# Scores of two tiles from seven block products: a fused cross-attention and feed-forward layer, re-ordered on all five engines

## The chip, the cores and the metric

The kernel runs on one core of a Trainium2 chip. The time is that of one execution on the device, in microseconds (us), the median of several runs. The core has five engines with instruction queues of their own: TensorE (PE; its weight loads are shown as PEld and overlap its matmuls), VectorE (DVE), ScalarE (ACT), GpSimd (POOL) and SyncE (SP), which here issues every DMA. Each queue is worked off strictly in order; semaphores tie the queues together.

## The reference

The input x has 8 batches of 1024 rows of 512 values; every batch has a context of 64 rows of 384 values. All is float32. Layer normalisation is without weights, and the linear layers of the second half quantise their input per row and their weights to -1, 0, 1.

```
def _xattn(x, context, Wq, Wk, Wv, Wo, bo):            # 8 heads of 64
    q, k, v = x @ Wq, context @ Wk, context @ Wv        # split into heads
    attn = softmax(einsum('bhsd,bhld->bhsl', q, k) * 64 ** -0.5)
    return merge_heads(einsum('bhsl,bhld->bhsd', attn, v)) @ Wo + bo

def _act_quant(x):
    scale = 127.0 / clip(max(abs(x), axis=-1), 1e-05)
    return clip(round(x * scale), -128.0, 127.0) / scale

def _bitlinear(x, w):
    return einsum('bsi,oi->bso', _act_quant(x), _weight_quant(w))

x = x + _xattn(_layernorm(x), ctx_768, Wq, Wk, Wv, Wo, bo)
h = silu(_bitlinear(_layernorm(x), w_gate)) * _bitlinear(_layernorm(x), w_up)   # 2048 wide
x = x + _bitlinear(h, w_down)
```

## The kernel before

**Tiles.** The 8192 rows are 64 tiles of 128 rows, 8 to a batch. `att[i]` is the attention of tile i, `ffn[i]` its feed-forward part, `pairs[i]` the tiles 2i and 2i+1.

**Attention through folded weights.** Context and weights are multiplied once per batch into two 512 x 512 float32 matrices: `score_w[b]` (x to the scores of 8 heads x 64 context rows) and `value_w[b]` (probabilities to the output). Three rooms hold each kind in turn, so those of later batches are made in the middle of the run, two batches at a time, in 8 steps each (`score_products`, `value_products`, L233 and L252, with copies by ScalarE). A tile's attention is then: transpose x, `scores` (four float32 matmuls of 512 columns, L360, each in two passes), subtract the maximum (L375, L377), exponentials (L382), sums and reciprocals (L386, L388), probabilities (L392), transpose them, and multiply by `value_w`. The transposes go through DMA: `split` (L310) separates the 16-bit halves on GpSimd, a DMA transpose follows (L312), and `join` (L319) puts the halves together, on ScalarE for x and on GpSimd for the probabilities p.

**Seven products for a pair's output.** Two tiles side by side are a 2 x 2 block problem: left blocks are pieces of p of 128 rows x 256, right blocks those of `value_w[b]`, 256 x 256. `Pair.product` (L454) computes the eight block products as seven, from five sums of left blocks (`Pair.sum`, L452, GpSimd, 128 x 256 each) and from sums of the weight blocks made once per batch (`value_sum`, L430, L432 and L434 on GpSimd, L436 on VectorE). The products x1 to x4 pile up in one PSUM bank, z1 and z2 in another, y goes to the bank of z; after each product VectorE adds or subtracts the bank's content as it stands into a quarter of a tile's x (L479). So x2 can't start before x1's result has been read, nor x3 before x2's, x4 before x3's, z1 before y's, z2 before z1's.

**Feed-forward.** `stats` (L282, L284, on VectorE; then L289, L291, the inverse deviation, on GpSimd), `normalise` (L493), `scale_x` (L499 and three small ones), `quantise_x` (ScalarE rounds, L509; GpSimd shrinks to 16 bits, L513; DMA transpose). `gate_up(s)`, for s from 0 to 3: four fp8 matmuls for the gate and four for the up part (L536, 512 columns), then silu on ScalarE (L551), product on VectorE (L552), and after s = 1 and s = 3 the largest value of 1024 columns (L564). `scale_h` and `quantise_h` (L577, L579, DMA transpose in two halves), and `output`, the down product (16 matmuls, L587; result added by L591).

**The order of the work.** A list written by hand brings the weights in and the first six tiles through attention. Then the loop `for k in range(NU + 1)`, NU = 64, emits step k in one order that holds for all engines; nothing re-orders it. Step k runs the feed-forward part of tile k, the quantisation of tile k + 1, the down product of tile k - 1, and the scores and softmax of tile k + 6; x of tile k + 7 is transposed. Output products of a pair are spread over two steps, y, x1, z1, x2 in the even and x3, z2, x4 in the odd one. Each step switches ScalarE's function table to Exp and back to Silu (L890, L904). From step 53 on there are exceptions: `quantised(k)` prepares two tiles in steps 53, 54, 56 and 58 and none in some others, and `downs(k)` puts the down products one step later. Gate, up and down results take turns over six PSUM banks, the block products have two of their own.

Of the kernel before, what the change touches and what calls it, by code (L numbers as in the profile page):

```python
# [29 lines left out]
def xattn_ffn_kernel(  # L30
# [58 lines left out]
    six = const.tile([P, 2, P], F32, name="p_sum_6")  # L89
# [24 lines left out]
    p_sums = [sums_room[:, i].rearrange("p (c t) -> p c t", c=2) for i in range(4)] + [six]  # L114
    value_sums = [
        [sums_room[:, ts(2 + 3 * i + j, 2)] for j in range(3)] for i in range(2)
    ]
# [169 lines left out]
    def inverse_std(mv, name, gain):  # L287
        ve = small.tile([P, 1], F32, tag="ve", name=f"ve_{name}")
        nc.gpsimd.tensor_scalar(ve, mv[:, 1:2], EPS, gain, ALU.add, ALU.mult)  # L289
        rs = small.tile([P, 1], F32, tag="rs", name=f"rs_{name}", bufs=8)  # L290
        nc.gpsimd.tensor_tensor(rs, ve, neg_half, ALU.pow)  # L291
        return rs
# [15 lines left out]
    def split(src, name):  # L308
        halves = apool.tile([P, 2, D], U16, tag=f"{name[0]}2", name=f"split_{name}")
        nc.gpsimd.tensor_copy(halves, src.bitcast(U16).rearrange("p (d h) -> p h d", h=2))  # L310
        halves_t = apool.tile([P, 2 * ND, P], U16, tag=f"{name[0]}2_t", name=f"split_t_{name}")
        nc.sync.dma_start_transpose(out=halves_t, in_=halves.rearrange("p h d -> p (h d)"))  # L312
        return halves_t

    def join(copy, halves_t, name):
        whole = apool.tile(
            [P, ND, P], F32, tag=f"{name[0]}_t", name=f"{name[0]}_t_{name}", bufs=1 + (name[0] == "p")
# [8 lines left out]
    class Attention:  # L326
# [9 lines left out]
        def copy_x(self):  # L336
            self.x_t = apool.tile([P, ND, P], F32, tag="x_t", name=f"x_t_{self.name}")
            nc.scalar.copy(self.x_t, self.pt)

        def split_x(self):  # L340
            self.x = x_tile(self.i)
            self.x2_t = split(self.x, f"x_{self.name}")
# [4 lines left out]
        def split_p(self):  # L347
            self.p2_t = split(self.p.rearrange("p h l -> p (h l)"), f"p_{self.name}")
# [16 lines left out]
        def softmax(self, between):  # L365
            self.less_maximum()
            self.exponentials()
            between()
            self.sums()
            self.probabilities()  # L370

        def less_maximum(self):
            pm = self.pm.rearrange("p (h l) -> p h l", h=HEADS)
            mx = small.tile([P, HEADS], F32, tag="mx", name=f"mx_{self.name}")
            nc.vector.tensor_reduce(mx, pm, AX.X, ALU.max)  # L375
            self.p = apool.tile([P, HEADS, L], F32, tag="p", name=f"p_{self.name}", bufs=2)
# [46 lines left out]
    def block(b, i, j):  # L423
        return value_w[b][:, ts(i, 2), ts(j, 2 * P)]

    def value_sum(b, i):

        s6, s1, s7 = value_sums[b % 2]
        if i == 0:
            nc.gpsimd.tensor_tensor(s6, block(b, 0, 0), block(b, 0, 1), ALU.add)  # L430
        elif i == 1:
            nc.gpsimd.tensor_tensor(block(b, 0, 1), block(b, 0, 1), block(b, 1, 1), ALU.subtract)  # L432
        elif i == 2:
            nc.gpsimd.tensor_tensor(s1, block(b, 1, 1), s6, ALU.subtract)  # L434
        else:
            nc.vector.scalar_tensor_tensor(s7, s1, -1.0, block(b, 1, 0), ALU.mult, ALU.subtract)  # L436

    class Pair:
        def __init__(self, i):
            self.tiles = att[2 * i], att[2 * i + 1]  # L440
            self.b, self.name, self.banks = self.tiles[0].b, f"pair{i}", {}

        def p(self, t, i):
            return self.tiles[t].p_t[:, ts(i, 2), :]

        def sum(self, i):
            p11, p12, p21, p22 = (self.p(t, i) for t in range(2) for i in range(2))
            a, b, op = (
                (p11, p21, ALU.subtract), (p11, p22, ALU.add), (p11, p12, ALU.add),
                (p22, p12, ALU.subtract), (p21, p22, ALU.add),  # L450
            )[i]
            nc.gpsimd.tensor_tensor(p_sums[i], a, b, op)  # L452

        def product(self, which):  # L454
            s6, s1, s7 = value_sums[self.b % 2]
            p, w, first = {
                "x1": (self.p(0, 0), block(self.b, 0, 1), True),
                "x2": (p_sums[1], s1, False),
                "x3": (self.p(1, 1), s7, False),
                "x4": (p_sums[3], block(self.b, 1, 0), False),  # L460
                "z1": (p_sums[0], block(self.b, 0, 0), True),
                "z2": (p_sums[4], s6, False),
                "y": (p_sums[2], block(self.b, 1, 1), True),
# [4 lines left out]
            for c in range(2):  # L468
# [3 lines left out]
                )  # L472
            t, n, op = {
                "x1": (0, 1, ALU.add), "x2": (1, 1, ALU.add), "x3": (1, 0, ALU.subtract),
                "x4": (0, 0, ALU.subtract), "z1": (1, 0, ALU.subtract), "z2": (1, 1, ALU.add),
# [6 lines left out]
    class FeedForward:  # L482
# [90 lines left out]
        def quantise_h(self):  # L573
            self.hq_t = hq_t_rooms[self.i % 2]
            for i in range(2):
                h = self.h[i]
                nc.scalar.activation(h, h, AF.Identity, bias=magic, scale=self.scale)  # L577
                hq = hq_rooms[i]
                nc.gpsimd.tensor_scalar(  # L579
                    as_chunks(hq), in_chunks(h), -MAGIC, 1.0, ALU.add, ALU.mult  # L580
                )
                nc.sync.dma_start_transpose(out=self.hq_t[:, ts(i, NF // 2), :], in_=hq)
# [267 lines left out]
    loaded = LEAD // 2 + 1  # L850
# [3 lines left out]
    def quantised(k):  # L854
# [5 lines left out]
        return [NU - 2] if k == NU - 4 else []  # L860
# [12 lines left out]
    rounds["product"] = rounds["bank"]  # L873
    for k in range(NU + 1):
        f = ffn[k] if k < NU else None
        a = att[k + LEAD] if k + LEAD < NU else None
        prev = att[k + LEAD - 1] if k == 0 else None
        after = att[k + LEAD + 1] if k + LEAD + 1 < NU else None
        quant, extra = ([ffn[i] for i in quantised(k)] + [None, None])[:2]
        pair = pairs[(k + LEAD - 2) // 2] if 2 <= k <= NU - LEAD + 1 else None  # L880
        parts = [("y", "x1", "z1", "x2"), ("x3", "z2", "x4")][k % 2] if pair else ()
        if k % 2 == 0 and loaded < NU // 2:
            load_x(loaded)
            loaded += 1
        if quant:
            quant.stats()
        if k > 0 and a:
            ffn[k - 1].quantise_h()
        if a:
            nc.scalar.preload_act_table(AF.Exp)  # L890
        if after:
            if k > 0:
                after.split_x()
            after.stats()
        if a:
            a.scores(every)

        def part(i):
            return pair.product(parts[i]) if i < len(parts) else lambda: None

        def between():
            if k == 0:
                after.copy_x()
            nc.scalar.preload_act_table(AF.Silu)  # L904
            read()
            if quant:
                quant.normalise()

        if k == 0:
            prev.transpose_p()  # L910
            prev.copy_p()
            after.transpose_x()
        if a:
            read = part(0)
            a.softmax(between)
            a.split_p()
        elif quant:
            quant.normalise()
        if pair and k % 2 == 0:
            pair.sum(3)  # L920
            pair.sum(4)
        if prev:
# [106 lines left out]
```

## Time and profile before

| | |
|---|---|
| median of 3 runs | 1170.16 us (1169.85 to 1171.77) |
| the profiled execution | 1169.91 us, its span 1168.1 us |
| granted TensorE clock | 0.999 |
| TensorE busy | 1153.5 us, 99% of the span |
| VectorE, ScalarE, GpSimd busy | 899.2 us (77%), 727.8 us (62%), 695.8 us (60%) |
| DMA | 126.85 MB, 109 GB/s on average |
| two steps of the loop at 312.63 us | 33.63 us |

The span counts from the first to the last instruction. Busy times are unions of an engine's instructions. A matmul's end is modelled, so its length in the profile (3.60 us for eight passes) is longer than the distance to the next start (3.44 us); distances between starts are the safer measure. A line of the profile names an engine, a source line (L360), the operation, out<-in by the program's names, and the form. PSUM is read by VectorE and ScalarE only, so a bank is free again when their reading instruction has ended.

### The profile page before, as it was taken

What the parts mean: (1) busy time and instruction counts of PE and PEld (TensorE: products, weight loads), DVE (VectorE), ACT (ScalarE), POOL (GpSimd) and SP (SyncE); (2) the same over time, 40 slices, a digit from 0 to 9 for tenths busy, and PEclk for the clock granted to TensorE, in tenths of its full rate; (3) what the DMA queues carried; (4) which work ended last, traced back from release to release, by engine and by line L of the source; (5) the groups of instructions that cost most, each with busy time, mean ns of one, the idle gap of its engine ahead of it and who ended that gap; (6) DMA issues with size and microseconds to landing.
All of it is one profiled execution on the core that took longest, in us unless ns stands there. A gap on an engine that the chain in (4) does not pass through costs nothing.

```text
span 1168.1 us, 15462 instructions
## 1 busy us (share of the span) xinstructions
PE 1153.5 (99%) x4966; PEld 607.9 (52%) x4966; DVE 899.2 (77%) x1832; ACT 727.8 (62%) x851; POOL 695.8 (60%) x879
## 2 busy tenths in 40 slices
PE   7999999999999999999999999999999999999998
PEld 6544555455555555545555555545555555555544
DVE  5786877777888777777787777777788777888775
ACT  3885666666566665676666566666665666566443
POOL 0565766557666665656756666555766667675432
PEclk9999999999999999999999999999999999999999
DMA  9863455345355434344445445544455544553244
GB/s 352 251 158 75 96 96 109 86 95 109 91 99 113 108 92 95 91 91 107 98 102 99 109 91 95 98 101 96 97 101 95 115 97 102 98 117 76 52 92 98
DMA packets 320352, 126.85 MB, mean 109 GB/s; under 512 B 304784, under 2 KB 305552, under 8 KB 319760
## 3 DMA queue, kind: packets, MB, share of 16 engines
q1 hardware_dynamic: 320272, 125.88, 48.7%
q8 instruction: 39, 0.64, 0.3%
q14 instruction: 41, 0.34, 0.1%
HBM read 34.08 MB, written 16.78 MB: 44 GB/s over the span
## 4 chain that ended last, share of the span: by engine, by line
PE 94%; DVE 1%; DMA 1%; POOL 1%; issue 1%; ACT 0%; SPq 0%; DVEq 0%; POOLq 0%; ACTq 0%
PE scores_a L360 18%; PE g_f L536 18%; PE u_f L536 18%; PE down_f L587 18%; PE x_pair L469 9%; PE z_pair L469 4%; PE y_pair L469 2%; PE attn_a L408 2%; PE score_ps L240 1%; PE value_ps L258 1%; PE k_late L203 1%; PE v_late L203 1%; DMA split_t_p_a<-split_p_a 1%; DMA arena<-in_L_xattn_Wk_dram 0%; PE k L203 0%
## 5 line engine op out<-in xcount | busy, mean ns | idle before, releaser
L536 PEld LDWEIGHTS <-xq_t_f 128*128 128x128 bf16 x1728 | 169.0, 98 | 189.8 <-DMA xq_t_f<-xq_f 1.9
L587 PE MATMUL down_f<-arena,room 128*128 128x512 fp8e4 x1008 | 227.9, 379 | 0.0
L551 ACT ACTIVATE ln_room<-g_f,dq_x_f 128x512 f32<-128x512 f32 x216 | 148.1, 686 | 125.0 <-PE g_f L536 116.7
L536 PE MATMUL g_f<-wg_t,xq_t_f 128*128 128x512 fp8e4 x864 | 221.7, 379 | 1.1 <-DMA xq_t_f<-xq_f 0.5
L536 PE MATMUL u_f<-arena,xq_t_f 128*128 128x512 fp8e4 x864 | 221.7, 379 | 0.0
L552 DVE SCALAR_TENSOR_TENSOR room<-u_f,dq_x_f,ln_room 128x512 f32<-128x512 f32 x216 | 161.2, 747 | 75.1 <-ACT ln_room L551 49.4
L360 PE MATMUL scores_a<-score_w,x_t_x_a 128*128 128x512 f32 x448 | 201.4, 592 | 0.0
L577 ACT ACTIVATE room<-room,magic,scale_h_f 128x1024 f32<-128x1024 f32 x126 | 149.4, 1233 | 81.2 <-DVE scale_h_f L299 81.0
L319 POOL COPY p_t_p_a<-split_t_p_a 128x1024 uint16<-128x1024 uint16 x58 | 77.5, 1335 | 152.1 <-DMA split_t_p_a<-split_p_a 148.8
L587 PEld LDWEIGHTS <-room 128*128 128x128 bf16 x1008 | 96.7, 98 | 123.8 <-issue 9.1
L579 POOL TENSOR_SCALAR room<-room 128x1024 bf16<-128x1024 f32 x126 | 138.7, 1119 | 31.7 <-ACT room L577 26.9
L564 DVE TENSOR_REDUCE am_h_f<-room 128x1 f32<-128x1024 f32 x126 | 153.2, 1216 | 2.3
L360 PEld LDWEIGHTS scores_a<-score_w,x_t_x_a 128*128 128x128 f32 x448 | 85.1, 190 | 88.4 <-issue 80.4
L382 ACT ACTIVATE p_a<-p_a,rs_a 128x512 f32<-128x512 f32 x64 | 46.2, 721 | 122.4 <-DVE p_a L377 120.5
L289 POOL TENSOR_SCALAR ve_f<-mv_f 128x1 f32<-128x1 f32 x64 | 12.2, 190 | 150.0 <-DVE mv_f L284 147.3
L591 DVE SCALAR_TENSOR_TENSOR x_room<-down_f,dq_h_f,x_room 128x512 f32<-128x512 f32 x63 | 47.2, 750 | 57.6 <-PE down_f L587 57.6
L375 DVE TENSOR_REDUCE mx_a<-scores_a 128x8 f32<-128x512 f32 x64 | 44.1, 689 | 60.3 <-PE scores_a L360 60.1
L392 POOL TENSOR_TENSOR p_a<-p_a,rc_a 128x512 f32<-128x512 f32 x64 | 66.9, 1045 | 35.0 <-DVE rc_a L388 25.1
L319 ACT COPY x_t_x_a<-split_t_x_a 128x1024 uint16<-128x1024 uint16 x56 | 74.5, 1331 | 6.7 <-DMA split_t_x_a<-split_x_a 6.7
L890 ACT ACT_TABLE_LOAD x58 | 74.4, 1283 | 1.0
L904 ACT ACT_TABLE_LOAD x58 | 74.4, 1283 | 1.0
L513 POOL TENSOR_SCALAR xq_f<-ln_room 128x512 bf16<-128x512 f32 x64 | 42.4, 662 | 34.8 <-ACT ln_room L509 22.1
(156 smaller groups left out, 1790.3 us busy)
## 6 DMA issues: line engine op xcount, KB each, us to landing
x_room<-in_x_dram SPq DMA_DIRECT2D x32, 512.0 KB, 4.1
out_dram<-x_room SPq DMA_DIRECT2D x31, 512.0 KB, 2.6
room<-in_L_ffn_w_gate_dram SPq DMA_DIRECT2D x3, 1024.0 KB, 14.3
room<-in_L_ffn_w_down_dram SPq DMA_DIRECT2D x2, 1024.0 KB, 6.9
room<-room SPq DMA_TRANSPOSE x126, 3.3
arena<-in_L_xattn_Wq_dram SPq DMA_DIRECT2D x1, 1024.0 KB, 7.1
score_w<-in_L_ffn_w_gate_dram SPq DMA_DIRECT2D x1, 1024.0 KB, 17.2
wo_sb<-in_L_xattn_Wo_dram SPq DMA_DIRECT2D x1, 1024.0 KB, 15.2
```

The source lines that it names most:

```text
L319: copy(whole.rearrange("p c t -> p (c t)").bitcast(U16).rearrange("p (m h) -> p h m", h=2), halves_t.rearrange("p (h c) t -> p h (c t)", h=2),
L360: nc.tensor.matmul(self.pm, lhsT=self.x_t[:, c, :], rhs=score_w[self.b][:, c, :], start=(c == 0), stop=(c == ND - 1),)
L469: nc.tensor.matmul(pm, lhsT=p[:, c, :], rhs=w[:, c, :], start=first and c == 0, stop=c == 1, skip_group_check=not first,)
L536: nc.tensor.matmul(ps, lhsT=self.xq_t[:, c, :], rhs=rhs.rearrange("p n (f e) -> p n e f", e=2)[:, :, c % 2], start=(c == 0), stop=(c == ND ...
L551: nc.scalar.activation(sg, pg, AF.Silu, scale=self.dq[:, 0:1])
L552: nc.vector.scalar_tensor_tensor(h[:, ts(s % 2, 512)], pu, self.dq[:, 1:2], sg, ALU.mult, ALU.mult)
L564: nc.vector.tensor_reduce(self.am[:, s // 2 : s // 2 + 1], h, AX.X, ALU.max, apply_absolute_value=True)
L577: nc.scalar.activation(h, h, AF.Identity, bias=magic, scale=self.scale)
L579: nc.gpsimd.tensor_scalar(as_chunks(hq), in_chunks(h), -MAGIC, 1.0, ALU.add, ALU.mult)
L587: nc.tensor.matmul(pm, lhsT=self.hq_t[:, f, :], rhs=every_other(wd_t[:, f // 2, :], f % 2), start=(f == 0), stop=(f == NF - 1),)
L890: nc.scalar.preload_act_table(AF.Exp)
L904: nc.scalar.preload_act_table(AF.Silu)
```

## The change

Scores get the scheme that the outputs have: `Seven` holds it for both, and a pair's scores are seven block products whose results go into the two tiles' p in SBUF: four of the seven (y, z1, x2, x4) by a ScalarE copy, three (x1, x3, z2) by a VectorE subtraction. The maximum and the subtraction then read p, not PSUM. Pairs 4 to 31 (tiles 8 to 63) go this way; tiles 6 and 7 are still scored alone in steps 0 and 1. Weight blocks are summed by four GpSimd instructions in one go (`weight_sums`), now for scores too. Even steps hold all seven score products of pair (k + 6)/2, odd steps all seven output products of pair (k + 3)/2. The exponentials of both tiles stand at the end of the even step, so that the function table changes twice in two steps; sums and probabilities are in the odd step. The pair sums on GpSimd are made at the end of the step before their products. x of tiles k + 8 and k + 9 is split in even steps and joined in the even and the next odd one. In even steps the quantisation of x now stands between the second and the third quarter of the step, in odd ones at the end as before.

```diff
+    def weight_sums(w, sums):
+        w11, w12, w21, w22 = (block(w, i, j) for i in range(2) for j in range(2))
+        nc.gpsimd.tensor_tensor(sums[0], w11, w12, ALU.add)
+        nc.gpsimd.tensor_tensor(w12, w22, w12, ALU.subtract)
+        nc.gpsimd.tensor_tensor(sums[1], sums[0], w22, ALU.subtract)
+        nc.gpsimd.tensor_tensor(sums[2], w21, sums[1], ALU.subtract)
...
+    class Seven:
...
+        def add(self, order):
+            p11, p12, p21, p22 = (self.left(t, i) for t in range(2) for i in range(2))
+            for i in order:
+                a, b, op = (
+                    (p11, p21, ALU.subtract), (p11, p22, ALU.add), (p11, p12, ALU.add),
+                    (p12, p22, ALU.subtract), (p21, p22, ALU.add),
+                )[i]
+                nc.gpsimd.tensor_tensor(block_sums[i], a, b, op)
...
+        def scores(self, which):
+            pm = self.seven.product(which)
...
+            to = self.tiles[t].p.rearrange("p h l -> p (h l)")[:, ts(n, 2 * P)]
+            if which in ("y", "z1", "x2", "x4"):
+                return lambda: nc.scalar.copy(to, pm)
+            if which == "x1":
+                return lambda: nc.vector.tensor_tensor(to, to, pm, ALU.subtract)
+            return lambda: nc.vector.tensor_tensor(to, pm, to, ALU.subtract)
...
     for k in range(NU + 1):
...
+        after = att[k + LEAD + 2] if k + LEAD + 2 < NU else None
+        scored = pairs[(k + LEAD) // 2] if even and FIRST <= (k + LEAD) // 2 < NU // 2 else None
+        soft = pairs[(k + LEAD - 1) // 2] if not even and FIRST <= (k + LEAD - 1) // 2 < NU // 2 else None
+        joined = pairs[(k + LEAD - 2) // 2] if even and FIRST <= (k + LEAD - 2) // 2 < NU // 2 else None
+        done = pairs[(k + 3) // 2] if not even and 3 <= k < NU - 6 else None
+        if k == NU - 6:
+            done = pairs[-1]
...
+        b, at = divmod(k + LEAD + 2, NT)
+        if quant and not soft and k != NU - 6:
+            quant.stats()
...
+        if not late or scored:
+            round_next(1 if scored or soft else 2)
+        if joined and k < NU - 6:
+            joined.tiles[0].join_p()
+        if after and even:
+            after.split_x()
+        if at == 4 and b < B:
+            weight_sums(value_w[b], value_sums)
...
+        part("y")()
+        if scored:
+            round_next(1)
+        part("x1")()
+        if soft:
+            soft.tiles[1].sums()
+            soft.tiles[1].probabilities()
+            soft.tiles[1].split_p()
+            if quant:
+                quant.stats()
+        early = quant and not soft and k != NU - 6
+        if early and not alone:
+            quant.normalise()
+            quant.scale_x()
         if f:
-            f.gate_up(0)
-            if not a:
-                part(0)()
+            if k != NU - 6:
+                f.gate_up(0)
             f.intermediate(0)
+            round_next(2)
...
+        part("z1")()
+        part("x2")()
+        if early:
+            quant.quantise_x()
+        if soft:
+            soft.tiles[0].sums()
+            soft.tiles[0].probabilities()
+        if after and not even:
+            after.join_x()
...
+            f.intermediate(1)
+        part("x3")()
+        part("z2")()
+        if soft:
+            soft.tiles[1].join_p()
+            soft.tiles[0].split_p("px"[k == NU - 7])
+            if k == NU - 7:
+                soft.tiles[0].join_p()
+        if after:
+            after.stats()
+        if scored:
+            t = scored.tiles[1]
+            t.less_maximum(t.p)
...
+        if not even and 5 + k // 2 < NU // 2:
+            load_x(5 + k // 2)
         if f:
             f.gate_up(2)
             f.intermediate(2)
+        if quant and not early:
+            quant.normalise()
+            quant.scale_x()
+        part("x4")()
...
+        if after and even:
             after.join_x()
+        if scored:
+            t = scored.tiles[0]
+            t.less_maximum(t.p)
...
             f.gate_up(3)
-            f.intermediate(3)
+            f.gated(3)
...
+        if even and 2 <= k < NU - 6 or k == NU - 7:
+            following = pairs[(k + 5) // 2]
+            following.start_output()
+            following.seven.add((2, 0))
+        elif not even and k < NU - 8:
+            following = pairs[(k + LEAD + 1) // 2]
+            following.start_scores()
+            following.seven.add((2, 0))
...
+        for q in (None if early else quant, extra):
             if q:
                 q.quantise_x()
+        if following:
+            following.seven.add((1, 4, 3))
+        ready = [scored.tiles[1], scored.tiles[0]] if scored else [att[LEAD + 1]] if k == 1 else []
+        if ready:
+            nc.scalar.preload_act_table(AF.Exp)
+            for t in ready:
+                t.exponentials()
+            nc.scalar.preload_act_table(AF.Silu)
+        if f:
+            f.largest(3)
...
+        if after and even:
+            att[after.i + 1].split_x()
+        if at == 0 and 0 < k and b < B:
+            weight_sums(score_w[b], score_sums)
         if f:
             f.scale_h()
```

Ahead of the loop `load_x(4)` and `weight_sums(score_w[1], score_sums)` are added, and in step 1 `weight_sums(value_w[0], value_sums)`. Joined x has two buffers instead of one, the inverse deviation 12 instead of 8. `quantise_h(i)` now does one half of h at a call.

## The prediction

> **What bounds the kernel now.** I read first the page's busy times, then TensorE in order of time, stretches of several steps, the waits, and last the rows by shape, which give the prices.
>
> ```profile
> span 1168.1 us, 15462 instructions
> ...
> PE 1153.5 (99%) x4966; PEld 607.9 (52%) x4966; DVE 899.2 (77%) x1832; ACT 727.8 (62%) x851; POOL 695.8 (60%) x879
> ```
>
> TensorE is busy 99% of the span. An overlapping queue can hide small waits in such a number, so the order of time has to confirm it (start, length, group):
>
> ```profile
> 316.00 3.60 PE L360 MATMUL scores_a<-score_w,x_t_x_a 128*128 128x512 f32 x8
> 319.44 1.03 PE L469 MATMUL x_pair<-arena,p_t_p_a 128*128 128x256 f32 x4
> 320.30 1.03 PE L536 MATMUL g_f<-wg_t,xq_t_f 128*128 128x512 fp8e4 x4
> ...
> 328.94 3.62 PE L587 MATMUL down_f<-arena,room 128*128 128x512 fp8e4 x16
> 332.39 3.60 PE L360 MATMUL scores_a<-score_w,x_t_x_a 128*128 128x512 f32 x8
> 335.82 1.03 PE L469 MATMUL y_pair<-value_w,arena 128*128 128x256 f32 x4
> ...
> 1104.30 1.03 PE L469 MATMUL x_pair<-arena,p_t_p_a 128*128 128x256 f32 x4
> 1105.17 1.03 PE L469 MATMUL z_pair<-arena,p_sum 128*128 128x256 f32 x4
> ```
>
> Take start to start, not the modelled length. A block product or four fp8 matmuls take one unit, 0.864 us (319.44 to 320.30); a down 3.45; one tile's scores 3.44. Two block products in succession, a new situation in the change, also take one unit each (1104.30 to 1105.17). Nothing stands between the groups.
>
> ```profile
> 312.63:346.26 33.63, 33.63 (x142) 17.74 (x141) 27.16 (x56) 20.53 (x23) 21.20 (x28) 1.00 0.50 102
> 860.00:896.00 36.00, 36.00 (x152) 19.19 (x151) 29.61 (x61) 22.00 (x24) 23.35 (x31) 1.00 0.52 103
> ```
>
> Columns: stretch, its length, then busy PE, weight loads, VectorE (DVE), ScalarE (ACT), GpSimd (POOL), granted clock. Two steps take 33.63 us, all TensorE's, at full clock; VectorE has 27.2 of it (81%), GpSimd 21.2 (63%). So the bound is the count of matmul units, and an engine beside it matters once its chain comes later than its reader on TensorE.
>
> **The change, part by part.** The sum goes against the profiled execution, 1169.9 us, 0.25 below the median of 1170.16.
>
> *TensorE.* Of 64 tiles, 56 (28 pairs) get seven products: 7 x 0.864 = 6.05 us for 2 x 3.435 = 6.87. That is 0.82 a pair, 28 x 0.82 = 23.0 us, and two steps become 32.8. With no stall: 1169.9 - 23.0 = 1146.9.
>
> *Each step's clock.* With 0 at the first product: y 0, x1 0.86, gate/up 0 at 1.73, z1 3.46, x2 4.32, gate/up 1 5.18, x3 6.91, z2 7.78, gate/up 2 8.64, x4 10.37, gate/up 3 11.23, down 12.96, end 16.42. A result can be read 0.2 after its group (scores ended 319.44, L375 began 319.64).
>
> *ScalarE* gains four copies a pair (0.38 each by the rows of L250) and loses two of four table loads (1.28 each): -1.0 us a pair. Even step, in its new order: round h to 1.45, copy y to 1.85, round h to 3.1, silu 3.8, copy z1 4.9, copy x2 5.8, round x 6.6, silu 7.3, silu 10.4, copy x4 11.8, join x 13.15, silu 13.85, Exp table 15.1, two exps 16.6, Silu table 17.85. z1 needs y copied (1.85 against 3.46), x3 needs x2's copy (5.8 against 6.91): no wait.
>
> *VectorE* gains three subtractions a pair (0.41 each, row L479) and loses the fourth weight sum (0.68 per batch). Durations: L552 and L591 0.75, L564 1.22, statistics 0.86, normalise 0.90, x scale 1.19, softmax reductions 0.67 to 0.69. Even step: busy 14.6; it idles for the x2 copy, which stands ahead of silu 1, until 7.3; then L552 8.05, L564 9.3, x3 9.7 (x4 starts 10.37: margin 0.7), z2 10.1, statistics 11.0, maximum and subtraction 12.4, L552 13.15, the same for the other tile 14.55, L552 15.3, L564 16.5, scale of h 17.1. Odd step, from 0.8: busy 15.3, x2 read 5.8 (x3 6.91), x3 read 9.5 (x4 10.37), x scale 13.6, scale of h 16.6. Busy 29.9 of 32.8 us (91%), yet each lateness is absorbed within the next step: cost 0, margins 0.7 to 1.5 us. The two subtractions now read SBUF only. No row shows that beside a busy GpSimd; the nearest are L436 at 0.68 and, with GpSimd active, normalise:
>
> ```profile
> L493 DVE TENSOR_SCALAR ln_room<-x_room,mv_f,rs_f x64: 535/903/1452, 81.6 to 1131.5; 128x512 f32<-128x512 f32 x64
> ```
>
> (minimum, median, maximum ns.) I take L436, the nearer kind; the high end is 1.45, +0.76 each. [...]
>
> *GpSimd, pair sums.* Five sums more a pair, 0.738 each (L452): 3.7 us. Even step: inverse deviation 2.75 (it waits for VectorE's statistics, as now: 147.3 us of such waits in all), shrink h 3.9, join p 5.2, split x 6.2, shrink h 7.35, shrink x 8.0, idle for statistics until 11.0, then 11.9, five sums to 15.6, split x 16.6. Odd step: shrink 3.8, probabilities 4.85, split 5.9, statistics 6.7, shrink 7.8, probabilities 8.85, join p 10.25 (its transpose landed at 9.0), split 11.3, statistics 12.1, two sums 13.55, shrink x 14.95, three sums to 17.1. The next y needs sum 2 at 12.8, x2 sum 1: in time. The shrunk x lands 2.3 us after its issue (the row of its 54 transposes), at 17.3 = 0.9 in the next step, against gate/up 0 at 1.73: 0.8 us of margin, where now it is about four. Cost 0. On SP's queue the x load now stands after the odd step's p splits; 4.1 us to land, read five us into the next step: 0.
>
> *GpSimd, weight sums.* Now four in succession (L430, L432, L434: 1.27 to 1.28 each, 5.1 us) instead of three spread over three steps, and for scores too.
>
> ```profile
> L430 POOL TENSOR_TENSOR arena<-value_w x8: 1262/1268/1277, 107.0 to 971.9; 128x512 f32<-128x512 f32 x8
> ```
>
> The value sums stand in step 8n+4 between split x and the second shrink of h. That shrink ends at 12.6, its transpose needs 3.1 (the row of split p, equal in size), lands 15.7, and the second half of down starts 14.69: 1.0 us of stall, on every other engine too. Of the seven steps (4, 12, ... 52), 4, 20 and 36 have 1.15 us of score or value matmuls ahead of the down, which cover it: 4 x 1.0 = 4.0 us. The score sums end step 8n; the odd step starts GpSimd at 5.5, shrink x ends 17.1, lands 19.4 = 3.0, against 1.73: 1.25 us. Steps 8, 24, 40 are covered by the same 1.15 twice; 16, 32, 48 pay: 3.75 us. Bounds for both: 0 (should a transpose land early) and twice that.
>
> *Start and end.* In steps 0 to 2 the x transposes and sums come a step earlier; there TensorE idles some 1.6 us today (109.39, 115.12, 125.44), and by the same walk it idles about that again: 0, bounds -1.5 to +2. Steps 53, 54 and 56 prepare two feed-forward tiles, 2.95 us more VectorE each; with only 1.5 us of air a step they make z1 late behind y's read in 54, 55 and 57 (0.65 + 1.35 + 0.65), and step 58 has x2 and x3 in succession (0.7), where now this stall stands:
>
> ```profile
> 1093.87 1.10 PE L469 MATMUL z_pair<-value_w,arena 128*128 128x256 f32 x4 [0.83 <-DVE x_room L479]
> ```
>
> Sum 3.35 - 0.83 = 2.5; since the same double steps pass without any idle now, I take 2.0, bounds 0 to 4.
>
> *Sum.* 1146.9 + 4.0 + 3.75 + 2.0 = 1156.7 profiled, 1157.0 as a median.
>
> **The rivals.** *Every stall is hidden* (transposes land early, GpSimd waits less): 1147.2. For it: the walk's stalls are about 1 us and sit on 2.3 to 3.1 us medians of transposes. Against: GpSimd runs its list in order, and 5.1 us in one piece has no gap of that length to go into.
>
> *A wait repeats in the plain steps*: a margin of 0.7 to 0.8 (x3's read in the even step, the shrunk x at the start of the even one) is overdrawn by 0.3 in each pair: 28 x 0.3 = 8.4, 1165.4. For it: 91% on VectorE; against: today 81% costs TensorE nothing.
>
> *VectorE becomes the bound, and the kernel slower.* Place: the two SBUF subtractions and two normalisations of a pair, all beside GpSimd's sums. At 1.45 each VectorE has 29.9 + 2 x 0.76 + 2 x 0.55 = 32.5 us, with its forced idle of 2.1 a pair, 34.6. The 16 pairs of steps without weight products then lose 34.6 - 33.63 = 1.0 each (+15.5), the 12 with them keep -0.82 (-9.8): +5.7, and with the weight sums' 7.75 about 1183. It decides when VectorE's own period passes 33.63: by the walk it is 29.9 + 2.1 = 32.0, so 1.6 us more a pair. Against: 903 is the median, not 1452.
>
> **How the numbers follow.** A run of this kernel tells 0.2% (2.3 us) from no change. The forecast's own case (1150 to 1161) 0.50; all hidden (under 1150) 0.20; repeating wait (1161 to 1167.8) 0.13; within 0.2% 0.04; slower 0.13. Faster is 0.83. The range from 1147.0, the floor without stalls, to 1168.0 leaves out the slower case and a little of the next.
>
> **What would show it.** Right: TensorE's two steps at 32.8 between the sums' steps; gaps near 1.0 ahead of the second half of down in steps 12, 28, 44, 52 and ahead of gate/up 0 in 18, 34, 50; VectorE near 29.9 of 32.8; the probabilities' maximum no longer waiting for TensorE. Wrong: a gap in every step ahead of x3, x4 or z1 released by VectorE, or a block product longer than 0.864.

## The result and the profile after

The changed kernel takes 1182.3 us (median of 4 runs, 1180.5 to 1182.6) against 1170.0 (1169.9 to 1171.8) for the kernel before: 1.0098 times as long, 95% interval 1.0081 to 1.0116. It is 1.0% slower; 1157.0, 1.1% faster, was predicted.

The page of the changed kernel, its span and the line of busy times:

```profile
span 1180.8 us, 16657 instructions
...
PE 1140.5 (97%) x5302; PEld 674.0 (57%) x5302; DVE 959.6 (81%) x1908; ACT 693.4 (59%) x907; POOL 858.5 (73%) x1055
```

TensorE is busy for 13 us less (1153.5 before) and the span is 12.7 us longer, so some 26 us of idle time have come in. They aren't in the plain steps. The stretch view of two steps without weight sums (columns: stretch, its length, busy PE, weight loads, VectorE, ScalarE, GpSimd, clock):

```profile
344.66:377.46 32.80, 32.80 (x153) 20.05 (x152) 29.13 (x59) 19.28 (x26) 25.30 (x33) 1.00 0.48 104
```

Two steps take 32.80 us, all TensorE's, as predicted; VectorE is busy for 29.1 of them (29.9 predicted). The idle time is found in TensorE's groups by shape, whose last column is the idle time just ahead of the group and what ended it:

```profile
L611 PE MATMUL down_f<-arena,room 128*128 128x512 fp8e4 x1008 | 229.2, 380 | 6.3 <-DMA room<-room 6.3
L564 PE MATMUL u_f<-arena,xq_t_f 128*128 128x512 fp8e4 x864 | 223.0, 381 | 1.9 <-DVE p_a L375 1.9
L564 PE MATMUL g_f<-wg_t,xq_t_f 128*128 128x512 fp8e4 x864 | 222.8, 381 | 9.0 <-DMA xq_t_f<-xq_f 8.9
...
L465 PE MATMUL y_o_pair<-value_w,arena 128*128 128x256 f32 x116 | 30.8, 390 | 2.8 <-POOL arena L449 2.8
...
L465 PE MATMUL x_s_pair<-score_w,arena 128*128 128x256 f32 x112 | 28.9, 381 | 2.3 <-DVE p_a L497 2.3
```

Two transposes are the largest releasers (of h ahead of down, of the shrunk x ahead of the gate), with 6.3 and 8.9 us; before, the first released no idle time and the second 0.5 us. This view still understates the loss, because matmuls that run at a low clock count as busy (from 402.79 to 406.21 us TensorE is busy for all 3.42 us at a clock of 0.50). So the table counts from start to start: the distance between two groups less its plain value (0.864 us for four fp8 matmuls or a block product, 3.45 for a down), summed by place, low clock included; excesses under 0.12 us are left out, and the sums are good to about 0.2. The last column is span less these sums.

| kernel | median | span | steps 0 to 2 | ahead of down's second half (value sums' steps) | steps 9 to 50, ahead of gate/up 0 and y | from step 53 | span less these |
|---|---|---|---|---|---|---|---|
| before | 1170.0 | 1168.1 | 1.7 | 0 | 0 | 1.9 | 1164.5 |
| changed | 1182.3 | 1180.8 | 2.9 | 7.4 | 14.8 | 13.2 | 1142.5 |
| no weight sums in the loop | 1157.5 | 1155.5 | 2.9 | 0 | 0.5 | 9.8 | 1142.3 |
| sums in halves | 1162.4 | 1162.8 | 2.9 | 0 | 5.6 | 13.4 | 1140.9 |
| x load behind the transpose | 1173.0 | 1168.8 | 2.9 | 7.4 | 9.3 | 7.1 | 1142.1 |
| down ahead of y in step 58 | 1179.3 | 1177.5 | 2.9 | 7.5 | 16.7 | 10.0 | 1140.4 |
| halves + load | 1158.0 | 1156.7 | 2.9 | 0 | 0.8 | 11.2 | 1141.8 |
| halves + load + gate/up + single preparations | 1154.7 | 1153.8 | 2.9 | 0 | 1.1 | 7.5 | 1142.4 |

The last column shows that the gain was there: 1164.5 - 1142.5 = 22.0, and over all variants 22 to 24, against 23.0 predicted for the 28 pairs. The waits of the changed kernel, 38.3 against 3.6 before, outweigh it. The rest of the table comes from the experiments.

### The profile page after: what moved, and what is told of

It is laid out like the page before. It is cut to its first block, busy times and chain, and to the rows that moved or that the text cites. A ratio compares the mean times of both kernels' runs of the same rounds, so it can differ in the third digit from the quotient of the medians.

```text
span 1180.8 us, 16657 instructions
## 1 busy us (share of the span) xinstructions
PE 1140.5 (97%) x5302; PEld 674.0 (57%) x5302; DVE 959.6 (81%) x1908; ACT 693.4 (59%) x907; POOL 858.5 (73%) x1055
## 4 chain that ended last, share of the span: by engine, by line
PE 69%; DVE 11%; POOL 9%; DMA 6%; issue 3%; ACT 2%; SPq 0%; POOLq 0%; DVEq 0%; ACTq 0%
PE down_f L611 14%; PE g_f L564 13%; PE u_f L564 13%; PE x_o_pair L465 7%; PE x_s_pair L465 5%; PE z_o_pair L465 3%; PE z_s_pair L465 3%; DVE room L580 2%; PE y_o_pair L465 2%; DMA room<-room 2%; PE scores_a L360 2%; DVE am_h_f L592 2%; DMA xq_t_f<-xq_f 2%; POOL room L605 2%; DVE ln_room L521 1%
## 5 line engine op out<-in xcount | busy, mean ns | idle before, releaser
L604 ACT ACTIVATE room<-room,magic,scale_h_f 128x1024 f32<-128x1024 f32 x126 | 155.3, 1239 | 63.9 <-DVE scale_h_f L299 54.6
L605 POOL TENSOR_SCALAR room<-room 128x1024 bf16<-128x1024 f32 x126 | 145.1, 1154 | 60.4 <-ACT room L604 54.7
L319 POOL COPY p_t_p_a<-split_t_p_a 128x1024 uint16<-128x1024 uint16 x58 | 83.1, 1433 | 11.9 <-DMA split_t_p_a<-split_p_a 10.5
L521 DVE TENSOR_SCALAR ln_room<-x_room,mv_f,rs_f 128x512 f32<-128x512 f32 x64 | 67.5, 1054 | 18.8 <-POOL rs_f L291 18.8
L289 POOL TENSOR_SCALAR ve_a<-mv_a 128x1 f32<-128x1 f32 x64 | 15.5, 242 | 86.0 <-DVE mv_a L284 82.8
L537 ACT ACTIVATE ln_room<-ln_room,magic,scale_x_f 128x512 f32<-128x512 f32 x64 | 52.1, 814 | 22.1 <-DVE scale_x_f L299 18.2
L507 DVE TENSOR_TENSOR x_room<-x_room,x_o_pair 128x256 f32<-128x256 f32 x116 | 48.3, 416 | 20.4 <-PE x_o_pair L465 19.4
L449 POOL TENSOR_TENSOR arena<-p_t_p_a,p_t_p_a 128x256 f32<-128x256 f32 x87 | 63.7, 745 | 0.0
L310 POOL COPY split_p_a<-p_a 128x1024 uint16<-128x1024 uint16 x58 | 61.1, 1053 | 1.9
L449 POOL TENSOR_TENSOR arena<-x_t_x_a,x_t_x_a 128x256 f32<-128x256 f32 x84 | 62.2, 741 | 0.0
## 6 DMA issues: line engine op xcount, KB each, us to landing
score_w<-in_L_ffn_w_gate_dram SPq DMA_DIRECT2D x1, 1024.0 KB, 17.5
```

What stands on the lines that cost most here:

```text
L319: copy(whole.rearrange("p c t -> p (c t)").bitcast(U16).rearrange("p (m h) -> p h m", h=2), halves_t.rearrange("p (h c) t -> p h (c t)", h=2),
L449: nc.gpsimd.tensor_tensor(block_sums[i], a, b, op)
L521: nc.vector.tensor_scalar(self.ln, self.x, self.mv[:, 0:1], self.rs, ALU.subtract, ALU.mult)
L605: nc.gpsimd.tensor_scalar(as_chunks(hq), in_chunks(h), -MAGIC, 1.0, ALU.add, ALU.mult)
```

## The experiments

The theory (A): the gain is real and the GpSimd weight sums, 5.1 us in one piece, make the waits. The rivals: (B) VectorE and GpSimd are too full in general, so that the waits would come anyhow; (C) part of the waits is made on SP's queue, where the 512 KB x load now stands right ahead of the transpose of the shrunk x. The end of the loop is a question of its own.

### Without the weight sums in the loop

```diff
-        if at == 4 and b < B:
-            weight_sums(value_w[b], value_sums)
...
-        if at == 0 and 0 < k and b < B:
-            weight_sums(score_w[b], score_sums)
```

> The changed kernel without the weight sums inside the loop (value sums of steps 8n+4, score sums of steps 8n); the output is therefore not the reference's, since later batches use stale sums. Nothing else is touched. Theory A (the sums in one piece of 5.1 us on GpSimd make the stalls ahead of the second half of down in steps 12, 28, 44, 52 and ahead of gate/up 0 in steps 18, 34, 50, with the low clock behind them): the 7.4 + 14.8 us that these places lost over the plain cadence go, 1182.3 - 21 = about 1161. Theory B (GpSimd and VectorE are too full in general, 73% and 81% busy, and the stalls would come somewhere anyway): 1172 to 1180. Theory C (the activation transposes land late because the 512 KB x load stands ahead of them on SP's queue): the score stalls of some 2.4 us shrink but do not vanish, about 1165.

Measured 1157.5 us, 0.9891 times the kernel before (0.9878 to 0.9905). All waits in steps 3 to 52 are gone but one of 0.5 us. (The time is below theory A's 1161 because the low clock of step 58 stayed away in this profile, 3.2 us.) So they need the sums: GpSimd and VectorE carry all the other work of the change without holding up TensorE. This run also takes work off GpSimd, so it doesn't yet tell one long piece (A) from too much work (B); the next one keeps the work as it is.

### The same sums in two halves

```diff
+        if summed:
+            weight_sums(*summed, halves=(0,))
         if after:
             after.stats()
...
-        if at == 0 and 0 < k and b < B:
-            weight_sums(score_w[b], score_sums)
+        if summed:
+            weight_sums(*summed, halves=(1,))
```

The first half is `sums[0]` and the difference into w12, the second `sums[1]` and `sums[2]`; the call in steps 8n+4 ahead of the products goes as well.

> The same four weight sums, but in two halves of 2.55 us: the first two ahead of the statistics of the even step, where GpSimd waits for VectorE, the last two at the end of the step. The work on GpSimd is unchanged. Theory A (one piece is the cause): nearly all of the 22 us goes, 1160 to 1164, below the kernel before (1170). Theory B (too much work in general): the stalls stay in sum, 1176 to 1183.

Measured 1162.4 us, 0.9932 (0.9918 to 0.9946): 20 us less for the same instructions, so (B) falls. GpSimd in step 16, in order of time:

```profile
370.73 1.27 POOL L429 TENSOR_TENSOR arena<-score_w 128x512 f32<-128x512 f32 x1 [0.86 <-PE z_s_pair L467]
372.08 1.27 POOL L430 TENSOR_TENSOR score_w<-score_w 128x512 f32<-128x512 f32 x1
373.43 0.51 POOL L289 TENSOR_SCALAR ve_a<-mv_a 128x1 f32<-128x1 f32 x1
...
379.48 1.28 POOL L432 TENSOR_TENSOR arena<-arena,score_w 128x512 f32<-128x512 f32 x1
380.84 1.27 POOL L433 TENSOR_TENSOR arena<-score_w,arena 128x512 f32<-128x512 f32 x1
382.19 1.14 POOL L607 TENSOR_SCALAR room<-room 128x1024 bf16<-128x1024 f32 x1
```

The first half fills time in which GpSimd waited for VectorE's statistics (2.73 us of idle time ahead of L289 at this place in the changed kernel), so only 2.55 us are pushed into the next step. The waits ahead of down vanish. Those ahead of gate/up 0 shrink from some 2.5 to 1.1 us but stay, and waits of 0.7 and 1.0 us come in steps 14 and 30, which (A) alone does not explain. With the x load moved as well (below) all of these fall to 0.3 us or less. One thing the run doesn't separate: the value sums have changed not only their length but their place, since none of them stands ahead of the shrink of h any more. For the score sums the second half kept its place, so there it is the length that counts.

### The x load behind the transpose

```diff
-        if not even and 5 + k // 2 < NU // 2:
-            load_x(5 + k // 2)
...
         for q in (None if early else quant, extra):
             if q:
                 q.quantise_x()
+        if not even and 5 + k // 2 < NU // 2:
+            load_x(5 + k // 2)
```

> The 512 KB load of x in odd steps is issued behind the transpose of the shrunk x instead of ahead of it on SP's queue. Theory C (the transpose lands 0.8 us late, 3.1 instead of 2.3 us, because of the load): the small waits of 0.15 to 0.46 us in steps 10, 14, 26, 42 go and each of the three large ones ahead of gate/up 0 shrinks by 0.8: -3.7 us, 1178.6; to -7 us where the low clock goes with them. Theory A alone (only the sums' length counts): within 1 us of 1182.3.

Measured 1173.0 us (1170.6 to 1174.3), 1.0018 (1.0010 to 1.0027): 9.3 us less, more than (C) expected; the profiled run is the shortest of its runs. First SP's queue and TensorE of the changed kernel around the start of step 18, then the same of this one:

```profile
396.66 0.53 SPq L162 DMA_DIRECT2D x_room<-in_x_dram  x1
398.40 1.20 SPq L550 DMA_TRANSPOSE xq_t_f<-xq_f  x1
```

```profile
398.18 1.03 PE L465 MATMUL x_s_pair<-score_w,x_t_x_a 128*128 128x256 f32 x4
401.57 1.04 PE L564 MATMUL g_f<-wg_t,xq_t_f 128*128 128x512 fp8e4 x4 [2.36 <-DMA xq_t_f<-xq_f]
402.45 1.56 PE L564 MATMUL u_f<-arena,xq_t_f 128*128 128x512 fp8e4 x4
403.81 1.91 PE L465 MATMUL z_s_pair<-score_w,arena 128*128 128x256 f32 x4
```

```profile
397.40 1.19 SPq L550 DMA_TRANSPOSE xq_t_f<-xq_f  x1
398.68 0.53 SPq L162 DMA_DIRECT2D x_room<-in_x_dram  x1
```

```profile
397.19 1.03 PE L465 MATMUL x_s_pair<-score_w,x_t_x_a 128*128 128x256 f32 x4
399.83 1.04 PE L564 MATMUL g_f<-wg_t,xq_t_f 128*128 128x512 fp8e4 x4 [1.61 <-DMA xq_t_f<-xq_f]
```

From the issue of the transpose to the gate it is 3.17 us behind the load and 2.43 without it ahead. The three long waits ahead of gate/up 0 shrink by 0.75 to 0.81 us each, the short ones (1.3 us in four steps) go, and after step 18's shorter wait there is no low clock any more (1.7 us in the changed kernel: 1.91 us for the z product at 403.81 instead of 1.03). Together that is the 5.5 us that this column of the table loses. The other 6.1 us of the profiled run lie at the end: one transpose took 3.2 us instead of 4.9 there (see below), and the low clock behind that wait stayed away. That part is not the load's doing, as far as the profile shows, so of the 9.3 us some 5.5 can be put down to the load, within the 3.7 to 7 that (C) gave.

### Down ahead of y in step 58

```diff
             f.gate_up(0)
             f.gate_up(1)
+            ffn[k - 2].output()
         part("y")()
...
-        return {late: [], NU - 1: [NU - 3, NU - 2], NU: [NU - 1]}.get(k, [k - 2])
+        return {late: [], NU - 6: [], NU - 1: [NU - 3, NU - 2], NU: [NU - 1]}.get(k, [k - 2])
```

> In step 58 the down product of tile 56 (3.45 us of TensorE) stands ahead of the pair's y product instead of at the step's end. In the changed kernel y waits there 2.83 us for a pair sum, and the products behind it run at a low clock, 3.5 us more. If this place is what the tail loses most by and TensorE has nothing else to do there: 1182.3 - 6 = about 1176, and the low clock goes too. If the chain of the last pair's reads on VectorE sets the end of the tail anyway, the gain is under 1 us.

Measured 1179.3 us, 1.0081 (1.0067 to 1.0095): 3.0 us less, between the two. The wait of y and the low clock are gone, but gate and up of the next steps then wait for VectorE, which has the reads of x and the products of h in a row: 1.98 + 1.30 + 1.40 us. Half of the gain was only moved.

### Both edits of the loop, with and without the down

> The three edits together: weight sums in halves, x load behind the transpose, down of tile 56 ahead of y in step 58. Theory A + C (the sums' length and the load's place add up, each with its own place): the spread sums' 1162.4 less the waits that its profile still has ahead of gate/up 0 in steps 10, 14, 18, 30, 34, 50 and 54 (0.5 to 1.2 us each, 6.5 in all), less 2 to 4 in step 58: 1152 to 1154. Rival (the later load only moves the collision to the transposes of h in the next step, or to the split of x that reads it): gaps appear ahead of the second half of down or ahead of the score products, 1157 or more.

With the three edits 1157.0 us, 0.9884 (0.9869 to 0.9899): better than either kernel, but 3 us over the expectation. In its steps 58 and 59 TensorE still loses 5.7 us, 2.0 and 1.3 of them in two waits of step 59, with the low clock behind the second: the down ahead of y mostly moved the wait.

> Only the two edits in the loop: weight sums in halves, x load behind the transpose; step 58 as in the changed kernel. If the down ahead of y only moved the wait (with three edits, steps 58 and 59 still waited 5.7 us), the time is within 2 us of that run's 1157.0. If it was worth the 3 us that it gave alone, 1160. The sums of waits in steps 2 to 52 should be under 2 us against 25 in the changed kernel.

With the two edits of the loop alone 1158.0 us, 0.9894 (0.9875 to 0.9913). So beside them the down ahead of y is worth 1 us at most, not 3, and the two intervals overlap. The sum of waits in steps 3 to 52 is 0.8 us. (A) and (C) together explain the loop: one piece of 5.1 us and one transfer in the wrong place. In the table's two columns for the loop the halves alone take off 16.6 us, the load alone 5.5 and both 21.4, so there the two nearly add up. The medians (20, 9 and 24 us) don't, because part of the 9 lies at the end.

### The preparations at the end

In steps 53, 54 and 56 two feed-forward tiles are prepared at once. Two orders with fewer of these, the first together with the three edits and a changed order in step 1:

```diff
-        late = {NU - 11: 10, NU - 10: 8, NU - 8: 6, NU - 6: 4}
-        if k in late:
-            return [NU - late[k], NU - late[k] + 1]
+        if k == NU - 11:
+            return [NU - 10, NU - 9]
+        if k == NU - 6:
+            return [NU - 4, NU - 3]
+        return [k + 2] if k < NU - 6 else {NU - 5: [NU - 2], NU - 4: [NU - 1]}.get(k, [])
...
             quant.normalise()
-            quant.scale_x()
             alone.less_maximum()
+            quant.scale_x()
```

> The three edits, and two more at the ends: from step 53 on only one step prepares two tiles at once (53), and steps 54 to 57 one each, instead of two in 53, 54 and 56; in step 1 the maximum of the lone tile stands ahead of the scale of x instead of behind it. If VectorE's double preparations make the waits ahead of x4 in step 54 (1.7 us) and ahead of x in step 56 (1.3 us): both go, and with 1 us from the start the time is 3 to 4 below the run with three edits, 1149 to 1151. Rival (VectorE has to do that work in these steps anyway, so the wait only moves to steps 57 to 60): within 1 us of the run with three edits.

Measured 1155.5 us, 0.9870 (0.9853 to 0.9886), 1.5 less than with the three edits alone, not 3 to 4, and the intervals overlap. The waits of step 55 (1.35 and 0.43; the expectation put them in step 56) go, that of step 54 stays, and the edit in step 1 lost 0.7 us instead of winning: the wait of 2.1 us for the lone tile is gone, but down, y, z1 and x4 behind it wait 3.6 us in sum instead of 0.9.

The second order has its one double step in 55 (`if k < NU - 9: return [k + 1]`, then `k == NU - 9` with two tiles), with the two edits of the loop:

> The two edits in the loop, and the double preparations of the tail (steps 53, 54 and 56) replaced by one double in step 55 and single ones in 53, 54, 56 and 57. If the waits ahead of x4 in step 54 (1.7 us), of x3 in step 56 (1.3) come from VectorE's double preparations, both go: 3 us below the run with the two edits alone. If VectorE's load of these steps as a whole makes them, a wait of that size shows up in steps 55 to 57 instead and the time is the same within 1 us.

Measured 1156.8 us, 0.9883 (0.9868 to 0.9898), which is not clear of the 1158.0 without it. The trace says more than the time. TensorE in step 54 with the double steps of the change, and in step 56 with the one in 55:

```profile
1014.08 1.03 PE L566 MATMUL u_f<-arena,score_w 128*128 128x512 fp8e4 x4
1016.62 1.10 PE L467 MATMUL x_s_pair<-score_w,arena 128*128 128x256 f32 x4 [1.51 <-DVE p_a L499]
```

```profile
1046.98 1.03 PE L566 MATMUL u_f<-arena,score_w 128*128 128x512 fp8e4 x4
1049.54 1.10 PE L467 MATMUL x_s_pair<-score_w,arena 128*128 128x256 f32 x4 [1.53 <-POOL arena L451]
```

The wait moved with the double step, from the step behind 53 to the step behind 55, and kept its size. It belongs to the double preparation in an odd step; the releaser named is x3's read in the one case and a pair sum in the other.

### Gate and up as cover: the fastest of the versions measured

Instead of the down, the third quarter of gate and up goes ahead of y in step 58, with the double step in 53 only:

```diff
             f.gate_up(0)
             f.gate_up(1)
+            f.gate_up(2)
         part("y")()
```

> The two edits in the loop, single preparations in steps 54 to 57 (a double one in 53), and in step 58 the third quarter of gate and up ahead of y as cover (1.73 us of TensorE). If the wait of y for the pair sum is the tail's cost, it shrinks by 1.7 us, and with the 1.3 us of step 56 the time is 2 to 3 below the run with the two edits alone. If VectorE's chain of reads behind y sets the end, the same within 1 us.

Measured 1154.7 us (1153.9 to 1155.6), 0.9868 (0.9852 to 0.9885): 1.3% faster than the kernel before and 2.3% faster than the change. Its y waits 1.28 us instead of 3.05, as expected, and at full clock. Its interval overlaps that of the two edits alone (0.9875 to 0.9913), so how much of the difference is real is open.

### The changed kernel once more

> The changed kernel once more, unchanged, for a second profile. If the low clock behind a long TensorE wait depends on the wait's length alone, the stretches with clock 0.5 to 0.7 come at the same places as in the first profile (after the waits of step 18, 50 and 58, not of 34). If it also depends on when the wait falls, some of them move or vanish while the waits stay within 0.1 us.

One run, 1182.25 us. The long waits are within 0.25 us of the first profile's, and the low clock stands behind the same three, in steps 18, 50 and 58, and not behind that of step 34, which at 2.59 us is longer than that of step 18 (2.52). So the length alone does not decide here; where the waits of steps 18 and 34 fell in the first profile is in the last section. The same is seen in step 58 without the weight sums in the loop, and with the sums in halves and the load moved; TensorE around y, first the former:

```profile
1073.48 1.03 PE L564 MATMUL u_f<-arena,score_w 128*128 128x512 fp8e4 x4
1077.38 1.13 PE L465 MATMUL y_o_pair<-value_w,arena 128*128 128x256 f32 x4 [2.87 <-POOL arena L449]
1078.35 1.03 PE L465 MATMUL x_o_pair<-value_w,p_t_p_a 128*128 128x256 f32 x4
```

```profile
1072.99 1.03 PE L566 MATMUL u_f<-arena,score_w 128*128 128x512 fp8e4 x4
1076.90 1.92 PE L467 MATMUL y_o_pair<-value_w,arena 128*128 128x256 f32 x4 [2.88 <-POOL arena L451]
1078.61 1.91 PE L467 MATMUL x_o_pair<-value_w,p_t_p_a 128*128 128x256 f32 x4
```

Idle 2.87 and 2.88 us; the products behind take 0.97 us from start to start in the one and 1.71 in the other.

## Why the prediction was wrong, point by point

**The steps that held.** The unit and the plain step (32.80 us), the gain of 23.0 us (22 to 24 by the table), the end of the maximum's wait for TensorE, and the places of the waits: ahead of the second half of down in steps 12, 28, 44 and 52, ahead of gate/up 0 in 18, 34 and 50. The walk along GpSimd's list was good to half a microsecond: the shrunk x of step 17 was ready 17.5 us after that step's first product (17.1 predicted). The sizes failed: 9.75 us of new waits were predicted and 38.3 - 3.6 = 34.7 came, which less 23.0 is +11.7, against +12.2 by the medians.

**Score sums, 3.75 predicted, 14.8 measured: the step that failed most.** The x load on SP's queue was put at nothing. The sentence was that the x load "now stands after the odd step's p splits; 4.1 us to land, read five us into the next step: 0". It asked whether the load comes in time for its own reader, not what it stands ahead of. It stands ahead of the transpose with the smallest margin of the step: 0.75 to 0.81 us on each long wait, and 1.3 us in steps 10, 14, 26 and 42, which were priced at nothing. The other missing terms are the low clock behind the waits of steps 18 and 50 (1.7 + 1.4 us), and in step 49 a transpose of p of 5.0 us, which made y of step 50 wait 1.5 us and the gate 1.1 us more than in step 34. With the load moved, step 18's wait is 1.78, against 1.25 predicted: that is what the term itself was off by.

**Value sums, 4.0 predicted, 7.4 measured: the mechanism right, the size off.** Each wait is 1.5 to 1.6 instead of 1.0, and the three steps called covered wait 0.37. In step 12, GpSimd and then VectorE:

```profile
307.43 1.27 POOL L431 TENSOR_TENSOR arena<-value_w,arena 128x512 f32<-128x512 f32 x1
308.67 1.57 POOL L605 TENSOR_SCALAR room<-room 128x1024 bf16<-128x1024 f32 x1
```

```profile
308.50 0.75 DVE L375 TENSOR_TENSOR p_a<-p_a,mx_a 128x512 f32<-128x512 f32 x1
```

The shrink of h takes 1.57 us where its median is 1.12. It starts inside the subtraction of the maximum, which still had 0.58 us to run. All shrinks of h at this line (minimum, median, maximum in ns):

```profile
L605 POOL TENSOR_SCALAR room<-room x126: 1087/1123/1586, 110.9 to 1161.9; 128x1024 bf16<-128x1024 f32 x126
```

Seven of the 126 start inside such a subtraction, those of steps 4, 12, 20 and so on to 52, and they take 1.57 to 1.59 us; the longest of the other 119 takes 1.33. With the sums in halves none starts so, and none takes more than 1.30. So the excess of 0.45 goes with the overlap, and it is the missing half microsecond of each wait. That the one instruction holds up the other is argued from this; no run took the overlap away by itself.

**The two subtractions that read SBUF: the row was nearer than the high end.** They are the instructions of L375, one for each tile of a pair, which subtract the maximum; they were taken at 0.68 us:

```profile
L375 DVE TENSOR_TENSOR p_a<-p_a,mx_a x56: 691/758/1266, 134.8 to 1077.0; 128x512 f32<-128x512 f32 x56
L375 DVE TENSOR_TENSOR p_a<-scores_a,mx_a x8: 691/692/693, 41.4 to 115.2; 128x512 f32<-128x512 f32 x8
```

Those that read PSUM (`scores_a`) take 0.69 us each time, those that read SBUF 0.69 to 1.27, with a median of 0.76: 0.08 more than the row of 0.68, and below the high end of 1.45. What makes the longer ones long, no run shows. The plain steps have no wait ahead of x3 (TensorE is busy for all of their 32.80 us). What cost time here is GpSimd's shrink, 0.45 us a time, in the one place where it had no margin.

**The end, 2.0 more predicted, 11.3 more measured (13.2 against 1.9).** The waits of the double steps were foreseen (0.65 + 1.35 + 0.65 in steps 54, 55 and 57) and came as 2.5 in step 54 and 1.8 in step 55. The largest was not: y of step 58 waits 2.99 us for a pair sum, and the low clock and the reads behind it cost 3.9 more. That sum stands behind a join, and the join behind a DMA transpose issued at the end of step 57, a chain that the prediction never walked. It isn't the weight sums' doing: without them in the loop y waits 3.0 us there as well. Where that transpose took 3.2 instead of 4.9 us (the run with the later x load), y still waited 1.14.

**The start, 0 predicted, +1.2 measured** (2.9 against 1.7), inside its bounds.

**The rivals.** "VectorE becomes the bound" gave about 1183, close to the 1182.3 measured, but that is chance, since its mechanism did not occur: VectorE is busy for 29.1 us of two plain steps and TensorE never waits for it there. "A wait repeats in the plain steps" did not come either: its 0.3 us a pair was assumed, no run shows it, and two plain steps took 32.80 us without a wait. And "every stall is hidden" is what the loop does once both causes are out of it. The range to 1168.0 fell short because bounds were set term by term on each wait's length, and none for what follows a wait or for another queue.

## What to carry to other kernels

When an order is laid anew, look on every queue at what now stands directly ahead of the transfer with the least margin; that a moved transfer reaches its own reader in time is only half of the question. Work in one piece on an engine that goes through its list in order cost here what exceeded the gap it stood in: the same 5.1 us cut in two, the first half put where the engine was waiting anyway, cost under 1 us over the whole loop once the load was out of the way. And when a change removes work from the engine that bounds the kernel, price the waits it opens with a surcharge: behind three of the waits of the changed kernel the clock fell to 0.50, which cost 1.4 to some 3.2 us a time.

## What the runs showed of the hardware that was not expected

**The clock fell after some of the waits, and not after another of nearly the same length.** The stretch view of the changed kernel around the waits of step 18 (2.36 us idle) and step 34 (2.43 us idle); the second number is the length, the third the busy time of TensorE, and the last three are the clock, the DMA's share and its GB/s:

```profile
399.38:402.79 3.41, 1.22 (x6) 0.60 (x7) 1.76 (x2) 0.65 (x2) 3.16 (x6) 1.00 0.35 101
402.79:406.21 3.42, 3.42 (x10) 2.41 (x8) 1.91 (x6) 0.98 (x2) 3.23 (x3) 0.50 0.42 78
675.86:679.27 3.41, 1.81 (x9) 1.25 (x7) 1.96 (x4) 2.57 (x3) 3.16 (x7) 1.00 0.88 212
679.27:682.69 3.42, 2.59 (x12) 1.65 (x13) 2.75 (x6) 0.69 (x1) 3.34 (x4) 1.00 0.19 38
```

The borders of these stretches are not chosen freely. In this profile the stretches with a clock of 0.50 begin at 17.09, 402.79, 959.17 and 1099.11 us; the distances between them, 385.70, 556.38 and 139.94 us, are 113, 163 and 41 times 3.413 us. The first three last 3.41 us, the fourth 6.83. The lines above are cut on the grid that this gives. The wait of step 18 lies nearly whole in one stretch, which leaves TensorE 1.22 us of work in 3.41, and the clock of the next one is 0.50. The wait of step 34 is cut in two by the border at 679.27, both parts keep 1.81 us of work or more, and the clock stays at 1.00. The other two falls after the start follow stretches with 0.40 us of work (955.75 to 959.17, step 50) and 1.19 (1095.70 to 1099.11, step 58). From 30 us on, the least busy stretch that no fall follows has 1.49 (112.66 to 116.07).

So in this kernel an idle time of 2.36 us that lay nearly whole in one stretch had a fall behind it, and one of 2.43 us that was cut in two had none. These rows show where the falls stood; what brings them about was not shown, and no run varied the place of a wait by itself. The three falls cost 1.7, 1.4 and some 3.2 us, behind waits of 2.36, 3.57 and 2.83 us.

**A transpose of p that takes 5.0 us instead of 3.1.** In the changed kernel this befell those of steps 49 and 57 (5.0 and 4.9 us), ahead of two of its three longest waits. Each time a 16 KB packet of the instruction queue q8 began 2.9 us after the transpose's issue. The DMA view from 945.1 to 950.2 us, that queue's packet first, then the landing:

```profile
q8 instruction: 1, 0.02, 1.3%
...
split_t_p_a<-split_p_a SPq DMA_TRANSPOSE x1, 5.0
```

Twenty transposes of that kernel have such a packet begin 1 to 3 us after their issue: ten of them took 4.2 to 5.0 us, three 3.6 to 4.0, and seven the usual 2.4 to 3.1. Others without a packet took over 4 us too, such as the one issued at 955.56 (4.1). So the packet may be a cause but does not decide alone; no run was made for it, and the cause stays open.
